# Pairs of expert tiles with the weights held in the array: a mixture-of-experts kernel on one Trainium2 core

## The chip, the core and the metric

The kernel runs on one core of a Trainium2 chip. The core has a matrix engine (TensorE, PE in the profile, whose weight loads are shown as PEld), a vector engine (VectorE, DVE), an activation engine (ScalarE, ACT), a general one (GpSimd, POOL) and SyncE (SP), which here only issues DMAs. The engines run side by side, each through its own queue in program order, and wait for each other by semaphores. Sixteen DMA engines move data between DRAM and SBUF, the on-chip memory of 128 partitions. TensorE writes to PSUM, which is used in banks of 128 x 512 fp32 values. The metric is the device time of one launch in microseconds, as the median of several runs.

## The reference

There are 4096 tokens of width 256, fp32 throughout. A layer norm feeds two branches, and x + both is the result.

```python
xn = _layernorm(x)
x = x + attention(xn, W_in, W_out) + moe(xn, ...)
# attention: Chebyshev features of q and k, running sums over the tokens
num = (Tq * kv_beta).sum(axis=3); den = (Tq.sum(axis=-1) * k_beta).sum(axis=3)
# moe
normed = layernorm(hidden, ln_w, ln_b); xf = normed.reshape(-1, 256)
logits = xf @ router_w                       # 8 experts
top_idx = argmax(logits); top_score = sigmoid(max(logits))
for e in experts:
    w = where(top_idx == e, top_score, 0.0)[:, None]
    xe = xf * w
    routed += (silu(xe @ g[e]) * (xe @ u[e])) @ d[e]      # 256 -> 512 -> 256
shared = (silu(xf @ sh_gate) * (xf @ sh_up)) @ sh_down
return hidden + routed + shared
```

Each token goes to one expert, and its score multiplies the rows before gate and up.

## The kernel before

The tokens form 8 chunks of 512, that is 32 tiles of 128 rows. The front (`front`) normalizes each chunk, writes the normalized rows to `z_dram`, and makes a transposed copy for the shared expert (`xfT`) and one for attention (`xnT`). `route` then finds each token's expert and a slot for it in a table: every expert's tokens fill whole tiles of 128 slots, and what is left over goes in quarters of 32 rows. With `NFULL = 26` whole tiles and `NPART = 31` quarters there are `NJ = 34` tiles, the last 8 of them quartered, and `NI = 57` sets of weights to load. The table holds, for each slot, the row to take from `z_dram` (`take_i`), the row of `y_dram` to write (`give_i`), and the score (`slot_s`).

`expert(n, j)` runs a tile. SyncE loads the gate, up and down weights of its expert, or of its four experts (L1173 to L1181, 512 KB each). GpSimd gathers the 128 rows by an indirect DMA (L1183). TensorE transposes them (L1191), ScalarE applies the layer norm's weight and bias on the way out of PSUM (L1194). Gate and up are matmuls in which the 128 rows lie in the array and 512 weight columns move (L1201), so they come out with the rows on the partitions. ScalarE's silu and VectorE's product (L1207, L1209) take the score as a factor per partition. The result is transposed in four blocks (L1214, L1216), so that the down product (L1222, 256 columns moving) can have it in the array. A copy (L1225 or L1226) and an indirect DMA (L1229) write the rows to `y_dram`. Quartered tiles keep four experts side by side in 32-column groups of the array.

`shared(c, gate)` is the shared expert on a chunk: L924 for gate and up with 512 columns moving, L933 for the product, L942 for down. It has the weights in the array and the tokens moving, so its intermediate result needs no transpose. `attend(c, gate)` is attention on a chunk: the qkv products (L987), a long chain of VectorE operations up to L1117, and the output product (L1125). At the end, SyncE loads `y_dram` back, chunk by chunk (L1251), VectorE adds it (L1260), and the result is stored (L1264). The loads of `y_dram` wait for all scatters.

The order on each engine is written out by a planner before the launch. Every operation is an `op` with an engine, a planned cost in us, what it reads and writes, buffers to allocate and a priority; `Plan.order` starts what is ready, by priority and by its planned clock, and emits it. A gather is planned with 1.28 us of GpSimd and a landing time, a scatter likewise; each scatter writes a key of its own:

```python
op("POOL", 1.28, f, r=[yt, "table"], w=[("y", j)], nbytes=128 * KiB, prio=SCAT)
```

The semaphores themselves are added afterwards by the framework, from the memory that the instructions touch. Buffers come from pools: `w_p` for weight sets (8 places, two more once the transposed copies of the front are free, and more once attention has ended), `zt_p` for gathered rows, `sl_p` and `hm_p` for the intermediate results, `bank_p` for six PSUM banks. `hold` ties the start of the last two shared chunks to the up products of given expert tiles.

Of the kernel before, what the change touches and what calls it, by code (L numbers as in the profile page):

```python
# [11 lines left out]
F32 = mybir.dt.float32  # L12
I32 = mybir.dt.int32
AF = mybir.ActivationFunctionType
ALU = mybir.AluOpType
AX = mybir.AxisListType
# [4 lines left out]
P = 128  # L21
NB, S, D = 2, 2048, 256
# [11 lines left out]

NFULL = NTT - 3 * NE // 4
NPART = 4 * NTT + NE - 1 - 4 * NFULL
NJ = NFULL + (NPART + 3) // 4
NI = NFULL + NPART  # L40
GP = 2
EPS = 1e-5
EPS_DEN = 1e-7
# [212 lines left out]
def kernel(  # L256
# [23 lines left out]

    z_dram = dram.tile([NTOK, D], F32, name="z_dram")
    y_dram = dram.tile([NTOK, D], F32, name="y_dram")
    ratio_dram = dram.tile([NTT, P], F32, name="ratio_dram")
    xn_dram = [dram.tile([P, KD, CH], F32, name=f"xn_dram_{c}") for c in range(NC)]
    xf_dram = [dram.tile([P, KD, CH], F32, name=f"xf_dram_{c}") for c in range(NC)]
# [52 lines left out]
    def cut(n):  # L338
        nonlocal at
        at += n  # L340
        return wide[:, at - n : at]
# [1 line left out]
    ratio_p = Pool([cut(CH) for _ in range(4)])  # L343
    route_at = at
    at = 0
    sl_p = Pool([cut(FF) for _ in range(3)])
    hm_p = Pool([cut(FF) for _ in range(2)])
    zt_p = Pool([cut(D) for _ in range(NZT)])
    xt_p = Pool([cut(D) for _ in range(2)])
    yt_p = Pool([cut(D) for _ in range(NYT)])  # L350
# [339 lines left out]
    def route():  # L690
# [3 lines left out]
        def t2(name, n=NTT, p=P):  # L694
            return cut(n)[:p]
# [4 lines left out]
        iota = t2("iota", P)  # L700
        top, idx, pos, tok1, score, hi = (t2(n) for n in ("top", "idx", "pos", "to", "sc", "hi"))
        quart = t2("quart", 4 * NTT)
        end = t2("en", NE)
        m, w = t3("m"), t3("w")
        iota_i = wide[:, at - NTT * NE : at - NTT * NE + P].bitcast(I32)
        tok = wide[:, at - NTT : at].bitcast(I32)
        tot, incl, gt = t3("tot", NTT, NE), t3("incl", NTT, NE), t3("gt", NTT, NE)
        le = t2("le", NI * NE, 1).rearrange("p (j e) -> p j e", e=NE)
        ej = t2("ej", NI, 1)
        full, odd, first, wh, lft, lend, base, jump = (t2(n, NE) for n in ("fu", "od", "fi", "wh", "lf", "le", "ba", "ju"))  # L710
        it_e = iota[:, :NE].unsqueeze(1).to_broadcast([P, NTT, NE])
        assert at <= wide.shape[-1]

# [61 lines left out]

        def f():
            V.tensor_reduce(odd, over, AX.X, ALU.add)
            V.tensor_reduce(full, over.rearrange("p e (t q) -> p e t q", q=4)[:, :, :, 3], AX.X, ALU.add)
        op("DVE", 1.6, f, r=["gt"], w=["full"], prio=R)

        def f():

            V.tensor_tensor_scan(end, ones[:, :NE], full, 0.0, ALU.mult, ALU.add)
            V.tensor_tensor(first, end, full, ALU.subtract)
            V.tensor_scalar(end, end, float(NFULL), None, ALU.min)
            V.tensor_scalar(first, first, float(NFULL), None, ALU.min)
            V.tensor_tensor(wh, end, first, ALU.subtract)
            V.scalar_tensor_tensor(lft, wh, -4.0, odd, ALU.mult, ALU.add)
            V.tensor_tensor_scan(lend, ones[:, :NE], lft, 0.0, ALU.mult, ALU.add)
        op("DVE", 1.4, f, r=["full", "gt"], w=["ends"], prio=R)  # L790

        def f():

            V.tensor_scalar(base, first, float(P), None, ALU.mult)
            V.tensor_tensor(lft, lend, lft, ALU.subtract)
            V.tensor_scalar(lft, lft, float(QD), float(NFULL * P), ALU.mult, ALU.add)
            V.tensor_scalar(wh, wh, float(P), None, ALU.mult)
            V.tensor_tensor(jump, lft, wh, ALU.subtract)
            V.tensor_tensor(jump, jump, base, ALU.subtract)
            V.tensor_tensor(incl, incl, tot, ALU.subtract)  # L800
        op("DVE", 1.4, f, r=["ends"], w=["start"], prio=R)

        def f():
            V.tensor_tensor(
                incl, rank.t[:, : NTT * NE].rearrange("p (t e) -> p e t", e=NE), incl, ALU.add,
            )
            V.tensor_tensor(gt, incl, wh.unsqueeze(2).to_broadcast([P, NE, NTT]), ALU.is_ge)
            V.tensor_tensor(gt, gt, jump.unsqueeze(2).to_broadcast([P, NE, NTT]), ALU.mult)
        op("DVE", 1.3, f, r=["start", rank], w=["slots0"], prio=R)

        def f():
            V.tensor_tensor(gt, gt, incl, ALU.add)
            V.tensor_tensor(
                w, gt.rearrange("p e t -> p t e"), base.unsqueeze(1).to_broadcast([P, NTT, NE]), ALU.add
            )
            V.tensor_tensor(w, w, m, ALU.mult)
        op("DVE", 1.2, f, r=["slots0", "m"], w=["slots"], prio=R)

        def f():
            V.tensor_reduce(pos, w, AX.X, ALU.add)  # L820
# [1 line left out]

        def f():

            for a, b, e in ((0, NFULL, end), (NFULL, NI, lend)):
                V.tensor_tensor(
                    le[:, a:b, :], e[0:1, :].unsqueeze(1).to_broadcast([1, b - a, NE]),
                    iota[0:1, : b - a].unsqueeze(2).to_broadcast([1, b - a, NE]), ALU.is_le,
                )
            V.tensor_reduce(ej, le, AX.X, ALU.add)  # L830
            V.tensor_scalar(ej, ej, float(NE - 1), None, ALU.min)
            V.tensor_copy(expert_i, ej)
# [59 lines left out]
        def f():  # L892
# [5 lines left out]
            V.scalar_tensor_tensor(u, table.t[:, :NJ], -0.75, u, ALU.add, ALU.add)  # L898
            V.tensor_copy(give_i, u)  # L899
        op("DVE", 1.1, f, r=[table, ("xn_dram", NC - 1)], w=["table"], prio=R)  # L900

    route()


# [238 lines left out]
    for i in range(2):  # L1143
        b = Buf(xfT_p, f"V_{i}")
        b.users = 1
        op("SP", 0.01, lambda: None, alloc=[b], prio=ROUTE, after=list(spilled),
           grow=lambda b=b: w_p.add([b.t]))
    for i, (q, n) in enumerate(((zt_p, D), (sl_p, FF), (hm_p, FF), (yt_p, D))):
        b = Buf(tv_p, f"U_{i}")
        b.users = 1  # L1150
        op("SP", 0.01, lambda: None, alloc=[b], prio=EXQ, after=lasts[-KD:],
           grow=lambda b=b, q=q, n=n: q.add([b.t[:, :n]]))
# [1 line left out]

    y_ins, downs, ups = [], [], []

    def expert(n, j):
        e = 0.1 * n

        parts = [(j, slice(0, P))]  # L1160
        if j >= NFULL:
            h = NFULL + 4 * (j - NFULL)
            m = min(4, NI - h)
            parts = [(h + i, slice(i * QD, (i + 1) * QD if i < m - 1 else P)) for i in range(m)]
        sets = [[Buf(w_p, f"{n}_{j}_{i}") for n in ("wg", "wu", "wd")] for i in range(len(parts))]
        wgs, wus, wds = ([s[i] for s in sets] for i in range(3))
        zt, xT, sl, hmT, yt = (Buf(q, f"{n}_{j}") for n, q in (
            ("zt", zt_p), ("xT", xt_p), ("sl", sl_p), ("hmT", hm_p), ("yt", yt_p)))
        pz, pg, pu, ph, py = (Buf(bank_p, f"{n}_{j}") for n in ("pz", "eg", "eu", "ph", "py"))
        ev = []  # L1170


        for n, src, cost in ((0, gate_w, 0.85), (1, up_w, 0.45), (2, down_w, 0.45)):  # L1173
            for i, (h, _) in enumerate(parts):
                def f(h=h, i=i, n=n, src=src, b=sets[i][n]):
                    if n == 0:
                        ev.append(nc.values_load(expert_i[0:1, h : h + 1], engines=[SP], min_val=0, max_val=NE - 1))
                    S_.dma_start(out=b.t.rearrange("p (k f) -> p k f", k=KF if n == 2 else KD),
                                 in_=src[ds(ev[i], 1)].rearrange("o (k p) f -> p (o k) f", p=P))
                downs.append(op("SP", cost, f, r=["experts"] + [("z_dram", n) for n in range(NC)], w=[sets[i][n]],  # L1180
                                alloc=[sets[i][n]], nbytes=512 * KiB, prio=EXQ + e, after=downs[-1:]))  # L1181

        op("POOL", 1.28, lambda: G.indirect_dma_start(  # L1183
            out=zt.t, out_offset=None, in_=z_dram,
            in_offset=bass.IndirectOffsetOnAxis(ap=take_i[:, j : j + 1], axis=0),
            bounds_check=NTOK - 1, oob_is_err=False,
        ), r=["table"] + [("z_dram", c) for c in range(NC)], w=[zt], alloc=[zt], nbytes=1024 * KiB, prio=EXQ + e - 0.05)

        def f():
            for k in range(KD):  # L1190
# [34 lines left out]
        op("ACT", 0.4, lambda: A.copy(yt.t, py.t[:, :D]), r=[py], w=[yt], alloc=[yt], prio=EXQ,  # L1225
           alt=[("DVE", 0.42, lambda: V.tensor_copy(yt.t, py.t[:, :D]))])  # L1226

        def f():
            y_ins.append(G.indirect_dma_start(  # L1229
                out=y_dram, out_offset=bass.IndirectOffsetOnAxis(ap=give_i[:, j : j + 1], axis=0),  # L1230
                in_=yt.t, in_offset=None, bounds_check=NTOK - 1, oob_is_err=False,
            ).ins)
        op("POOL", 1.28, f, r=[yt, "table"], w=[("y", j)], nbytes=128 * KiB, prio=SCAT)


    tiles = sorted(range(NJ), key=lambda j: j if j < NFULL else 3.2 * (j - NFULL) + 1.5)
    for n, j in enumerate(tiles):
        expert(n, j)

    gate, hold = [], {NC - 2: ups[-14], NC - 1: ups[-4]}
    for c in range(NC):
        gate = [shared(c, gate + ([hold[c]] if c in hold else spilled if c > 1 else []))]

# [1 line left out]
    for c in range(NC):  # L1247
        b = Buf(w_p, f"y_{c}")

        def f(c=c, b=b):  # L1250
            ins = S_.dma_start(  # L1251
                out=b.t.rearrange("p (t d) -> p t d", t=NT),
                in_=y_dram[c * CH : (c + 1) * CH].rearrange("(t p) d -> p t d", p=P),
            ).ins
            for s in y_ins:
                tc.add_manual_dep(ins, s.name, mybir.DependencyInfo(
                    mybir.DependencyClass.Sync, mybir.DependencyReason.DATA))
# [49 lines left out]
```

## Time and profile before

| quantity | value |
|---|---|
| median of 3 runs | 570.56 us (570.54 to 570.64) |
| the profiled execution | 570.69 us, of which the span 569.0 us |
| ScalarE | 238.0 us busy, 42% |
| VectorE | 486.2 us busy, 85%; 90 to 96% between 100 and 500 us |
| DMA | 132.67 MB, mean 233 GB/s |
| L1201, whole tiles from `big` (128*128, 512 moving) | 148 records, mean 595 ns |
| L1222, whole tiles from `big` (128*128, 256 moving) | 168 records, mean 387 ns |
| L1214, transposes of the intermediate result | 136 records with both forms, 276 ns |
| granted TensorE clock | 1.00 in the 28 stretches of 20 us up to 560 us, 0.95 after |

A mean of TensorE is the duration of one record, which includes the time through the array; neighbouring records overlap, so what one costs in a row of its kind is the distance from start to start, and the chain of work in order of time shows that. An fp32 matmul leaves two records. "Idle before, and its releaser" says how long an engine stood still ahead of an instruction, and which event ended that.

### The profile page before, as it was taken

What the parts mean: (1) busy time and instruction counts of PE and PEld (TensorE: products, weight loads), DVE (VectorE), ACT (ScalarE), POOL (GpSimd) and SP (SyncE); (2) the same over time, 40 slices, a digit from 0 to 9 for tenths busy, and PEclk for the clock granted to TensorE, in tenths of its full rate; (3) what the DMA queues carried; (4) which work ended last, traced back from release to release, by engine and by line L of the source; (5) the groups of instructions that cost most, each with busy time, mean ns of one, the idle gap of its engine ahead of it and who ended that gap; (6) DMA issues with size and microseconds to landing.
All of it is one profiled execution on the core that took longest, in us unless ns stands there. A gap on an engine that the chain in (4) does not pass through costs nothing.

```text
span 569.0 us, 8176 instructions
## 1 busy us (share of the span) xinstructions
PE 563.1 (99%) x2691; PEld 305.4 (54%) x2691; DVE 486.2 (85%) x799; ACT 238.0 (42%) x469; POOL 99.7 (18%) x113
## 2 busy tenths in 40 slices
PE   8999999999999999999999999999999999999997
PEld 7564555665535555464445455464555644553655
DVE  6899899999999999999899998999999999931254
ACT  4779662012553362354236435424733543311110
POOL 4211000005021102212120322215031321210100
PEclk9999999999999999999999999999999999999999
DMA  8857651336249918893884699299679938991089
GB/s 283 275 164 259 223 222 37 126 123 243 74 141 365 333 47 268 304 352 93 297 288 165 219 348 363 53 353 336 234 224 308 388 106 285 380 373 67 10 271 328
DMA packets 87689, 132.67 MB, mean 233 GB/s; under 512 B 5681, under 2 KB 52063, under 8 KB 87648
## 3 DMA queue, kind: packets, MB, share of 16 engines
q1 hardware_dynamic: 83152, 121.65, 62.7%
q0 software_dynamic: 3952, 10.51, 5.3%
q8 instruction: 21, 0.34, 0.3%
q14 instruction: 20, 0.16, 0.1%
q10 hardware_dynamic: 544, 0.00, 0.1%
HBM read 113.26 MB, written 19.15 MB: 233 GB/s over the span
## 4 chain that ended last, share of the span: by engine, by line
PE 98%; DVE 1%; DMA 0%; ACT 0%; issue 0%; DVEq 0%
PE bank L1201 22%; PE bank L924 20%; PE bank L987 15%; PE bank L1222 11%; PE bank L942 10%; PE bank L1125 5%; PE bank L1214 3%; PE psk L1017 3%; PE psq L1017 3%; PE bank L1191 1%; PE psk L1030 1%; PE bank L554 1%; PE psk L1111 1%; PE bank L874 1%; PE bank L587 1%; PE bank L1098 0%
## 5 line engine op out<-in xcount | busy, mean ns | idle before, releaser
L1201 PE MATMUL bank<-big,wide 128*32 128x512 f32 (+1 forms) x344 | 102.9, 596 | 0.0
L1229 POOL DMA_INDIRECT y_dram<-wide,give_i x32 | 41.4, 1293 | 304.1 <-ACT wide L1225 152.1
L987 PE MATMUL bank<-xnT,w_in 128*128 128x512 f32 x192 | 86.7, 594 | 0.0
L1054 DVE TENSOR_TENSOR_SCAN tv<-ones,carry,tv 128x512 f32<-128x512 f32 x60 | 76.6, 1277 | 1.2
L924 PE MATMUL bank<-xfT,sg 128*128 128x512 f32 (+1 forms) x136 | 61.1, 574 | 1.1 <-ACT xfT L532 1.1
L924 PE MATMUL bank<-xfT,su 128*128 128x512 f32 (+1 forms) x136 | 61.0, 573 | 0.0
L1201 PEld LDWEIGHTS bank<-big,wide 128*32 128x32 f32 (+1 forms) x344 | 34.6, 144 | 45.9 <-issue 42.1
L1183 POOL DMA_INDIRECT wide<-z_dram,take_i x34 | 42.9, 1262 | 85.5 <-DVE give_i L899 72.6
L942 PE MATMUL bank<-sd,hT 128*128 128x256 f32 x256 | 57.5, 379 | 0.0
L987 PEld LDWEIGHTS bank<-xnT,w_in 128*128 128x128 f32 x192 | 35.6, 190 | 39.0 <-issue 35.9
L1222 PE MATMUL bank<-big,wide 128*32 128x256 f32 (+1 forms) x352 | 54.2, 384 | 0.0
L942 PEld LDWEIGHTS bank<-sd,hT 128*128 128x128 f32 x256 | 48.0, 190 | 8.7 <-issue 2.5
L931 ACT ACTIVATE hT<-bank 128x512 f32<-128x512 f32 x32 | 19.0, 596 | 77.7 <-PE bank L924 73.5
L1222 PEld LDWEIGHTS bank<-big,wide 128*32 128x32 f32 (+1 forms) x352 | 37.0, 148 | 19.6 <-issue 7.5
L1207 ACT ACTIVATE wide<-bank,slot_s 128x512 f32<-128x512 f32 x33 | 22.6, 686 | 58.7 <-PE bank L1201 58.6
L1201 PE MATMUL bank<-xfT,wide 128*32 128x512 f32 (+1 forms) x100 | 45.6, 597 | 0.0
L1074 DVE TENSOR_TENSOR o<-o,tv 128x512 f32<-128x512 f32 x64 | 44.2, 690 | 1.7
L1209 DVE SCALAR_TENSOR_TENSOR wide<-bank,slot_s,wide 128x512 f32<-128x512 f32 x33 | 24.5, 743 | 17.9 <-PE bank L1201 17.5
L924 PEld LDWEIGHTS bank<-xfT,sg 128*128 128x128 f32 x136 | 24.6, 190 | 26.8 <-issue 24.1
L924 PEld LDWEIGHTS bank<-xfT,su 128*128 128x128 f32 x136 | 24.6, 190 | 25.3 <-issue 23.8
L1009 DVE SCALAR_TENSOR_TENSOR T<-T 128x1024 f32<-128x1024 f32 x32 | 38.1, 1220 | 0.0
L958 DVE TENSOR_TENSOR X<-X,bank 128x512 f32<-128x512 f32 x31 | 21.1, 679 | 15.6 <-PE bank L942 9.3
(224 smaller groups left out, 859.2 us busy)
## 6 DMA issues: line engine op xcount, KB each, us to landing
big<-in_gate_w SPq DMA_DIRECT2D x45, 512.0 KB
big<-in_down_w SPq DMA_DIRECT2D x44, 512.0 KB
big<-in_up_w SPq DMA_DIRECT2D x41, 512.0 KB
xfT<-in_up_w SPq DMA_DIRECT2D x14, 512.0 KB
xfT<-in_gate_w SPq DMA_DIRECT2D x11, 512.0 KB
xfT<-in_down_w SPq DMA_DIRECT2D x9, 512.0 KB
z_dram<-big SPq DMA_DIRECT2D x8, 512.0 KB
X<-in_x SPq DMA_DIRECT2D x7, 512.0 KB
```

The costliest lines, as they stand in the source:

```text
L924: T_.matmul(b.t[:, cols], wt[:, k, ts(f, P)], vx(k)[:, cols], start=(k == 0), stop=(k == KD - 1))
L942: T_.matmul(po.t[:, ts(i, D)], hT[f].t[:, ts(tp * 2 + i, P)], sd[:, f, :], start=(f == 0), stop=(f == KF - 1))
L987: T_.matmul(pm.t, w_in[:, k, ds(i * D + g * P, P)], xnT.t[:, ts(k, CH)], start=(k == 0), stop=(k == KD - 1))
L1009: op("DVE", 1.27, lambda i=i, j=j, q=part: V.scalar_tensor_tensor(q[i](), q[j](), off[i], q[1](), ALU.subtract, ALU.mult), r=[(T, j)] + X2 ...
L1017: T_.matmul(pt.t[ts(i - 1, QD), :], heads[:, 24 - g * HB : 24 - g * HB + QD], half[i](side), start=(g == 0), stop=(g == KD - 1 and (i > KD ...
L1054: o_ = op("DVE", 1.25, lambda b=b, i=i, g=g: V.tensor_tensor_scan(b.t, ones[:, 0:1].to_broadcast([P, CH]), b.t, 0.0 if opening else old[:, ...
L1074: op("DVE", 0.66, lambda o=o, b=b: V.tensor_tensor(o(), o(), b.t, ALU.add), r=[b, ok], w=[ok], prio=p)
L1125: T_.matmul(pa.t[:, ts(i, D)], o2.t[:, ds(g * CH + (tp * 2 + i) * P, P)], w_out[:, g, :], start=(g == 0), stop=(g == KD - 1))
L1183: op("POOL", 1.28, lambda: G.indirect_dma_start(out=zt.t, out_offset=None, in_=z_dram, in_offset=bass.IndirectOffsetOnAxis(ap=take_i[:, j ...
L1201: T_.matmul(b.t[n, :], xT.t[:, ds(k * P + n.start, n.stop - n.start)], wt.t[:, ts(k, FF)], start=(k == 0), stop=(k == KD - 1), skip_group_ ...
L1222: T_.matmul(py.t[n, :D], hmT.t[:, ds(i * P + n.start, n.stop - n.start)], wd.t[:, ts(i, D)], start=(i == 0), stop=(i == KF - 1), skip_grou ...
L1229: y_ins.append(G.indirect_dma_start(out=y_dram, out_offset=bass.IndirectOffsetOnAxis(ap=give_i[:, j : j + 1], axis=0), in_=yt.t, in_offset ...
```

## The change

Whole tiles are now of two kinds. `NPAIR = 9` pairs hold 256 rows of one expert, `NONE = 8` single tiles are left, the quarters stay 31: 9 + 8 + 31 = 48 weight sets. `pair(n, j)` gathers two tiles, transposes them into one bank, and has the weight blocks in the array with the 256 rows moving (L1256 of the changed file). Gate and up so come out transposed and go straight into the down product (L1269). As a row's score now lies along the free dimension, it can't be a factor per partition: the scores of the pairs are transposed once after routing (L926), stored to `score_dram` (L930), loaded for each pair spread over all partitions (L1230), and multiplied into the rows by VectorE before gate and up (L1246). A pair ends in one copy (L1272, L1273) and two scatters (L1211). Single and quartered tiles run through `expert` as before; gather, scatter and the weight loads have become functions. Routing has one more kind of slot to assign. `sl_p` and `hm_p` become one pool `h_p`; one of the two places that `w_p` got early goes to `h_p` and `zt_p` instead. The order of the units and the two `hold` points are new.

```diff
+NPAIR = (4 * NTT - 7 * NE) // 8
+NONE = NFULL - 2 * NPAIR
...
-NI = NFULL + NPART
+NI = NPAIR + NONE + NPART
...
-    sl_p = Pool([cut(FF) for _ in range(3)])
-    hm_p = Pool([cut(FF) for _ in range(2)])
+    h_p = Pool([cut(FF) for _ in range(5)])
...
+        rows = Buf(bank_p, "rows")
+        op("PE", MT, lambda: T_.transpose(rows.t[: 2 * NPAIR, :P], slot_s[:, : 2 * NPAIR], ident), r=["table"], w=[rows],
+           alloc=[rows], prio=R)
+        row = lambda: both.t[: 2 * NPAIR, 256 : 256 + P]
+        op("ACT", 0.25, lambda: A.copy(row(), rows.t[: 2 * NPAIR, :P]), r=[rows], w=[(both, "row")], prio=R)
+        op("POOL", 1.0, lambda: G.dma_start(out=score_dram, in_=row()), r=[(both, "row")], w=["score_dram"],
+           nbytes=8 * KiB, prio=R)
...
-           grow=lambda b=b: w_p.add([b.t]))
+           grow=lambda b=b, i=i: w_p.add([b.t]) if i else (
+               h_p.add([b.t[:, :FF]]), zt_p.add([b.t[:, ds(FF + n * D, D)] for n in range(2)])))
...
+    def scatter(j, yt, src):
+        def f():
+            y_ins.append(G.indirect_dma_start(
+                out=y_dram, out_offset=bass.IndirectOffsetOnAxis(ap=give_i[:, j : j + 1], axis=0),
+                in_=src(), in_offset=None, bounds_check=NTOK - 1, oob_is_err=False,
+            ).ins)
+        op("POOL", 1.28, f, r=[yt, "table"], w=[("y", j)], nbytes=128 * KiB, prio=SCAT)
+
+    def pair(n, j):
...
+        weights(e, [j // 2], [ws])
+        for i in range(2):
+            gather(e, j + i, zts[i])
+        op("POOL", 1.0, lambda: G.dma_start(
+            out=sc.t.rearrange("p (i q) -> p i q", i=2),
+            in_=score_dram[j : j + 2].unsqueeze(0).to_broadcast([P, 2, P])),
+           r=["score_dram"], w=[sc], alloc=[sc], nbytes=128 * KiB, prio=EXQ + e - 0.04)
...
+            V.tensor_tensor(v, v, sc.t.unsqueeze(1).to_broadcast([P, KD, 2 * P]), ALU.mult)
...
+            def mm(b, wt, h=h):
+                for f in range(2):
+                    for k in range(KD):
+                        T_.matmul(b.t[:, ts(f, 2 * P)], wt.t[:, ds(k * FF + (2 * h + f) * P, P)], xT.t[:, ts(k, 2 * P)],
+                                  start=(k == 0), stop=(k == KD - 1))
...
+            op("ACT", 0.62, lambda sl=sl, pg=pg: A.activation(sl.t, pg.t, AF.Silu), r=[pg], w=[sl], alloc=[sl],
+               prio=EXQ, table="silu")
+            op("DVE", 0.69, lambda sl=sl, pu=pu: V.tensor_tensor(sl.t, sl.t, pu.t, ALU.mult), r=[pu, sl], w=[sl],
+               prio=EXQ)
...
+            def f(i=i):
+                for f in range(KF):
+                    T_.matmul(py.t[:, ts(i, D)], sls[f // 2].t[:, ds(f % 2 * 2 * P + i * P, P)], wd.t[:, ts(f, D)],
+                              start=(f == 0), stop=(f == KF - 1))
...
+        op("ACT", 0.6, lambda: A.copy(yt.t, py.t), r=[(py, 0), (py, 1)], w=[yt], alloc=[yt], prio=EXQ,
+           alt=[("DVE", 0.69, lambda: V.tensor_copy(yt.t, py.t))])
+        for i in range(2):
+            scatter(j + i, yt, lambda i=i: yt.t[:, ts(i, D)])
...
-    tiles = sorted(range(NJ), key=lambda j: j if j < NFULL else 3.2 * (j - NFULL) + 1.5)
+    units = [(3 * i, expert, 2 * NPAIR + i) for i in range(NONE)]
+    units += [(3 * i + 1, pair, 2 * i) for i in range(NPAIR)]
+    units += [(3.1 * (j - NFULL) + 1.2, expert, j) for j in range(NFULL, NJ)]
...
-    gate, hold = [], {NC - 2: ups[-14], NC - 1: ups[-4]}
+    gate, hold = [], {NC - 2: ups[-10], NC - 1: ups[-3]}
```

## The prediction

> **What bounds the kernel now.** I read the page's busy shares first, then TensorE's waits, then the chain of work in order of time, and last the queue of GpSimd (POOL) and the end of the run, because the change moves work there.
>
> ```profile
> PE 563.1 (99%) x2691; PEld 305.4 (54%) x2691; DVE 486.2 (85%) x799; ACT 238.0 (42%) x469; POOL 99.7 (18%) x113
> PE 98%; DVE 1%; DMA 0%; ACT 0%; issue 0%; DVEq 0%
> ...
> PE bank L924 <- ACT xfT L532: 1.1, 1, 1.1
> PE bank L384 <- POOL ones L289: 1.1, 1, 1.1
> ```
>
> The two wait lines are all of TensorE's waits, and both lie in the first 9 us. After that TensorE never stands still until 565.3 us, so up to there the time is a sum of TensorE instructions. The chain in order of time prices them (start, us, what; an fp32 matmul leaves two records, a transpose one):
>
> ```profile
> 446.24 0.44 PE bank L1214 x4
> 446.68 0.22 PE bank L1191 x2
> 446.90 1.72 PE bank L1201 x4
> 448.62 0.44 PE bank L1214 x4
> 449.05 1.73 PE bank L1222 x8
> ```
>
> A matmul with 512 moving columns takes 1.72/2 = 0.86 us (longer runs: 0.858), one with 256 takes 1.73/4 = 0.4325, a transpose 0.109.
>
> The end is bound twice. The last expert matmul ends at 537.7; 6.9 us of L942 and 20.65 us of the last shared chunk (13.73 + 6.92) follow, to 565.3. Beside them runs this stream:
>
> ```profile
> 536.77 0.98 POOL L1229 DMA_INDIRECT y_dram<-wide,give_i  x1 [10.40 <-DVE wide L1226]
> 539.94 0.98 POOL L1229 DMA_INDIRECT y_dram<-tv,give_i  x1 [2.19 <-DMA y_dram<-wide,give_i]
> ...
> 542.57 1.47 SPq L1251 DMA_DIRECT2D T<-y_dram  x3
> ...
> 549.86 16.76 SPq L1264 DMA_DIRECT2D out<-X  x10
> ```
>
> All eight loads of y_dram wait for the last scatter; the 8.4 MB of loads and stores then fill the DMA engines (share 1.09 to 1.10, 348 to 387 GB/s) from 545 to 566.
>
> **The change, part by part.**
>
> TensorE, from the order in which both programs queue their instructions: gate and up lose 72 matmuls of 512 (72 x 0.858 = 61.8 us) and gain 144 of 256 (144 x 0.4325 = 62.3): +0.5. 72 transposes of L1214 go (-7.9), one comes for the scores (+0.1). A step from a 32-column tile to a full one costs about 0.19 more (L1222 x8 takes 1.93 there, not 1.73) and the step back 0.13; there are two fewer of each: -0.6. Sum **-7.9 us**, all on the path. [...]
>
> VectorE: routing gains 11 operations on 128x8 (0.17 each), one reduction (about 0.35) and 3 on 128x256 (0.42): +3.5. Up to its last attention product it also has 9 score products (0.66 each from start to start), 16 products of 0.61 for 16 of 0.66, three copies fewer, two shared products earlier: +5.3. That product ended at
>
> ```profile
> 500.80 0.75 DVE L1117 TENSOR_TENSOR o<-o,bank 128x256 f32<-128x256 f32 x2
> ```
>
> TensorE took it up 1.2 us later (502.7). With +8.8 it ends near 510, and TensorE, 7.9 us lighter but with 6.9 us of L942 and other work moved ahead of it, wants it near 508: 0 to 2.5 us of wait if nothing else delays TensorE. VectorE's own 22 us of waits between 20 and 502 can absorb it; I take 0, 2.5 goes into the range.
>
> ScalarE: fewer and wider activations, 42% busy, nothing. Weights: 27 loads of 512 KB fewer, but one weight place fewer too (9 before the late ones come, 10 before).
>
> GpSimd is where I expect the loss. Its queue runs in order. It gains nine score loads (0.55 us each by L499) and one score store, harmless by themselves. But a pair ends in **two scatters in a row**, and a scatter waits until the one before it has landed, as here:
>
> ```profile
> 376.46 1.84 POOL L1229 DMA_INDIRECT y_dram<-wide,give_i  x1 [6.69 <-ACT carry L1060]
> 384.21 1.00 POOL L1229 DMA_INDIRECT y_dram<-wide,give_i  x1 [5.90 <-DMA y_dram<-wide,give_i]
> ...
> DMA to landing us min/median/max: 2.1/6.1/7.4
> ...
> DMA to landing us min/median/max: 3.6/5.9/7.3
> ```
>
> The planner knows nothing of that wait: it charges 1.28 us for a scatter and gives each its own key. The two last lines are scatters and gathers. Where the DMA share after the issue is above 1.0, scatters land in 5.9 to 7.4 us, mostly 6.2; near 0.6 in 4.1 to 5.4; with idle DMA in 2.1 to 2.4. Gathers: 5.6 to 7.3, 4.2 to 5.2, 3.6.
>
> In the changed order the fifth to eighth pair's first gather stands right behind the second scatter of the pair before. From that pair's last matmul to the next pair's first transposes TensorE has only: a quartered tile's up 1.85, spreading 0.3, transposes 0.22, one shared gate 1.72, transposes 0.44, three qkv products 5.15, the quartered tile's down 1.9 = 11.6 us (11.5 to 11.8 at the four places). The chain needs: wake-up and copy 0.85, scatter 1.27, its landing 6.2, scatter 1.27, gap 0.3, gather 1.05, its landing 4.8 = 15.7. So TensorE stands still 4.1 us, four times: **+16.4**. I take 6.2 for the scatter since the quartered tile's four down weights (2 MB) and the next units' sets are being loaded just then, and 4.8 for the gather since that load is running out. All contended (6.2, 6.0): 16.9, or +21. Half (4.5, 4.5): +8. Idle (2.2, 3.6, short issues): 10, nothing. Behind the waiting scatter also stand other scatters and score loads; none is needed sooner than the gather.
>
> [...]
>
> The end: the last unit is now a pair, and 6.9 us of L942 have moved ahead of its last matmul, T0. T0 to the last TensorE instruction is 20.65. The copy (0.69) and wake-up take 0.95, the first scatter and its landing 0.98 + 2.19, the second 0.98, its landing 1.65 as before: first y load at T0 + 6.8 (before: + 4.8). From first y load to the span's end took 569.0 - 542.57 = 26.4; about 0.5 of it was the last two stores waiting for L949, which now come in time: 25.9. So the span ends at T0 + 32.7; TensorE's own path would be T0 + 24.4.
>
> Sum: TensorE ends at 565.3 - 7.9 + 16.4 = 573.8, T0 = 553.2, span 585.9. The profiled execution took 570.69 against a span of 569.0, so 1.7 lies around it: **587.6 us**; that execution is 0.1 above the median of 570.56. I say 587.
>
> **The rivals.**
>
> 1. Only the end counts: the gathers arrive in time (idle DMA, or the 10% less traffic). T0 = 565.3 - 7.9 - 20.65 = 536.8, span 569.5, time 571.2; with VectorE's 2.5 us 573.7. For: POOL is 18% busy and no gather was late before. Against: the DMA share at such moments.
> 2. On the faster side: the two scatters of a pair do not wait for each other. They come from one tile, a form no row shows. Then neither stall exists and the end is 3.2 us shorter: 536.8 + 29.5 + 1.7 = 568.0. It decides when the end after T0 is under 30.9. Against: every scatter that followed another closely in the trace waited.
> 3. Weight places run short: a quartered tile wants eight at once for gate and up, and one of nine still holds the pair's down. One 512 KB load late (1.5 us at 348 GB/s) in each of eight rounds is +12 on top: about 599.
>
> That the change does not do what it says is excluded by the instruction counts.
>
> **How the numbers follow.** Forecast 0.62, with 4 x 2 to 4 x 5.3 us of stalls: 579 to 593. Rival one 0.18, rival two 0.10, rival three 0.10. The range must take in rival one and the forecast's contended end: 570.5 to 596. Within 0.2% (569.4 to 571.7), about what a measurement here can tell from no change, lies a part of rival one: 0.06. Faster is rival two and a little: 0.11. Slower 0.83.
>
> **What would show it.** Right: TensorE idle before the transposes of four pairs, some 4 us each, released by the gather; GpSimd waiting some 6 us before each second scatter; about 12 us between the last matmul and the end, before 3.7; matmuls of 256 at 0.43. Wrong: second scatters without a wait, TensorE without idle time, or idle time released by weight loads or VectorE.

## The result and the profile after

The changed kernel takes **579.41 us** (median of five runs, 579.15 to 582.9) against 570.64 us for the kernel before beside it (570.54 to 571.5): a ratio of **1.0168**, 95% interval 1.0138 to 1.0197. The forecast was 587. The profiled execution is the slowest of the five, 582.9 us with a span of 581.1, and so 3.5 us longer than the median. Sums below are made against its own span.

The busy shares of the changed kernel, and all of TensorE's waits after the first 9 us (line waited at, releaser: us in total, times, longest):

```profile
PE 556.4 (96%) x2764; PEld 325.2 (56%) x2764; DVE 491.7 (85%) x820; ACT 223.2 (38%) x429; POOL 103.4 (18%) x123
...
PE bank L1237 <- DMA xfT<-z_dram,take_i: 6.8, 3, 4.0
PE bank L1237 <- DMA wide<-z_dram,take_i: 1.6, 1, 1.6
```

TensorE is busy for 6.7 us less than before, and yet it ends later: it now waits four times, 8.4 us in all, each time at a pair's first transposes (L1237), each time for a gather. What GpSimd did ahead of the longest of these waits stands in its queue in order of time (start, us, what, idle time before and its releaser):

```profile
386.76 1.10 POOL L1211 DMA_INDIRECT y_dram<-xfT,give_i  x1 [14.30 <-ACT xfT L1272]
394.15 1.35 POOL L1211 DMA_INDIRECT y_dram<-xfT,give_i  x1 [6.29 <-DMA y_dram<-xfT,give_i]
395.80 1.61 POOL L1203 DMA_INDIRECT xfT<-z_dram,take_i  x1 [0.30 <-issue]
```

The second scatter of a pair waits 6.29 us for the landing of the first. The gather behind it had nothing to wait for itself (0.30 us, "issue") and simply left late. On TensorE the same stretch reads:

```profile
402.18 0.41 PE L1237 MATMUL bank<-ident,xfT 128*128 128x128 f32 x2 [4.03 <-DMA xfT<-z_dram,take_i]
402.42 2.62 PE L1305 MATMUL bank<-big,wide 128*128 128x512 f32 x4
404.83 0.63 PE L1295 MATMUL bank<-ident,wide 128*128 128x128 f32 x2
405.25 2.69 PE L1256 MATMUL bank<-wide,xfT 128*128 128x256 f32 x8
407.78 0.60 PE L1318 MATMUL bank<-ident,wide 128*128 128x128 f32 x4
408.21 1.89 PE L1256 MATMUL bank<-wide,big 128*128 128x256 f32 x8
```

The wait is 4.03 us, and then the work is slower: two groups (L1305 x4, L1256 x8) that take 1.88 and 1.89 us elsewhere take 2.62 and 2.69. More on that in the last section.

The end, first TensorE's chain, then the loads and stores on SP's queue:

```profile
543.53 3.45 PE bank L1269 x16
546.98 8.60 PE bank L955 x20
```

```profile
553.14 0.37 SPq L1352 DMA_DIRECT2D T<-y_dram  x1
553.62 2.33 SPq L1352 DMA_DIRECT2D big<-y_dram  x3
556.05 5.75 SPq L1352 DMA_DIRECT2D T<-y_dram  x4
561.89 13.39 SPq L1365 DMA_DIRECT2D out<-X  x10
```

The last expert matmul (L1269) ends at 547.0, the first load of y is issued 6.2 us later, and the span ends 28.0 us after that. TensorE's last matmul ended at 567.7, so 13.4 us follow in which VectorE ends its additions (until 570.9) and the stores go out; before, 3.7 us followed.

### The profile page after: what moved, and what is told of

Read it like the earlier page. It is cut to its first block, busy times and chain, and to the rows that moved or that the text cites. A ratio compares the mean times of both kernels' runs of the same rounds, so it can differ in the third digit from the quotient of the medians.

```text
span 581.1 us, 8153 instructions
## 1 busy us (share of the span) xinstructions
PE 556.4 (96%) x2764; PEld 325.2 (56%) x2764; DVE 491.7 (85%) x820; ACT 223.2 (38%) x429; POOL 103.4 (18%) x123
## 4 chain that ended last, share of the span: by engine, by line
PE 43%; issue 9%; DMA 6%; POOL 1%; ACT 1%; DVE 1%; POOLq 0%
PE bank L1256 7%; PE bank L1305 7%; PE bank L1018 6%; PE bank L955 5%; PE bank L1269 4%; PE bank L1326 4%; PE bank L1156 4%; DMA xfT<-z_dram,take_i 3%; PE bank L973 2%; DMA T<-y_dram 2%; PE psk L1048 1%; PE psq L1048 1%; POOL y_dram L1211 1%; DMA wide<-z_dram,take_i 1%; DMA y_dram<-wide,give_i 1%
## 5 line engine op out<-in xcount | busy, mean ns | idle before, releaser
L1018 PE MATMUL bank<-xnT,w_in 128*128 128x512 f32 x192 | 87.1, 594 | 0.0
L1211 POOL DMA_INDIRECT y_dram<-wide,give_i x32 | 38.3, 1198 | 205.8 <-ACT wide L1329 49.6
L1305 PE MATMUL bank<-big,wide 128*32 128x512 f32 (+2 forms) x280 | 63.3, 602 | 0.0
L973 PE MATMUL bank<-sd,hT 128*128 128x256 f32 x256 | 58.0, 381 | 0.0
L1018 PEld LDWEIGHTS bank<-xnT,w_in 128*128 128x128 f32 x192 | 35.4, 190 | 36.7 <-issue 34.5
L973 PEld LDWEIGHTS bank<-sd,hT 128*128 128x128 f32 x256 | 47.8, 190 | 9.5 <-issue 3.2
L1203 POOL DMA_INDIRECT wide<-z_dram,take_i x20 | 26.3, 1317 | 110.7 <-DVE wide L921 78.7
L1305 PEld LDWEIGHTS bank<-big,wide 128*32 128x32 f32 (+2 forms) x280 | 18.4, 128 | 30.3 <-issue 29.5
L964 DVE TENSOR_TENSOR hT<-hT,bank 128x512 f32<-128x512 f32 x32 | 21.8, 683 | 16.1 <-PE bank L955 15.1
L1091 ACT COPY carry<-tv 128x1 f32<-128x1 f32 x80 | 15.1, 189 | 49.7 <-DVE tv L1085 49.2
L1082 DVE TENSOR_TENSOR tv<-T 128x512 f32<-128x512 f32 x48 | 32.4, 674 | 0.1
L1026 ACT ACTIVATE T<-bank 128x512 f32<-128x512 f32 x32 | 19.0, 596 | 30.8 <-PE bank L1018 30.6
L1256 PE MATMUL bank<-wide,big 128*128 128x256 f32 x128 | 30.4, 382 | 0.0
```

Of the source, the lines that this page charges most:

```text
L973: T_.matmul(po.t[:, ts(i, D)], hT[f].t[:, ts(tp * 2 + i, P)], sd[:, f, :], start=(f == 0), stop=(f == KF - 1))
L1018: T_.matmul(pm.t, w_in[:, k, ds(i * D + g * P, P)], xnT.t[:, ts(k, CH)], start=(k == 0), stop=(k == KD - 1))
L1082: V.tensor_tensor(b.t, q[i](1), v(), ALU.mult)
L1203: op("POOL", 1.28, lambda: G.indirect_dma_start(out=zt.t, out_offset=None, in_=z_dram, in_offset=bass.IndirectOffsetOnAxis(ap=take_i[:, j ...
L1211: y_ins.append(G.indirect_dma_start(out=y_dram, out_offset=bass.IndirectOffsetOnAxis(ap=give_i[:, j : j + 1], axis=0), in_=src(), in_offse ...
L1256: T_.matmul(b.t[:, ts(f, 2 * P)], wt.t[:, ds(k * FF + (2 * h + f) * P, P)], xT.t[:, ts(k, 2 * P)], start=(k == 0), stop=(k == KD - 1))
```

## Experiments

Ten runs, each against the kernel before on the same chip (570.72 to 570.74 us).

| run | what differs from the changed kernel | median us | range |
|---|---|---|---|
| changed kernel | | 579.41 | 579.15 to 582.9 |
| e1_told | planner knows that a scatter waits for the last one | 575.90 | 574.82 to 577.27 |
| e2_side | a pair's second scatter goes to another tensor | 571.42 | 570.88 to 571.6 |
| e3_hold | shared chunk later | 575.40 | 573.85 to 575.72 |
| e4_both | e1_told and e3_hold | 570.27 | 569.15 to 572.41 |
| e5_told6 | e4_both, scatters planned to land in 6 us | 570.66 | 570.3 to 571.6 |
| e6_side_hold | e2_side and e3_hold | 567.86 | 567.06 to 568.48 |
| e7_no_scores | score loads and products left out | 581.08 | 580.04 to 581.95 |
| e8_told6_no_scores | the same on e5_told6 | 569.61 | 569.56 to 569.91 |
| e9_told6_end | e5_told6, last ten scatters as before | **565.88** | 565.58 to 566.17 |
| e10_told5_end | e9_told6_end with 5 us | 567.71 | 567.38 to 568.51 |

**The wait between a pair's scatters, taken away.** A second DRAM tensor removes what makes the second scatter wait; every instruction and the queue's order stay. The final loads read `z_dram`, so the experts' sum is left out of the result (the diff is shortened to its changed lines).

```diff
-                out=y_dram, out_offset=bass.IndirectOffsetOnAxis(ap=give_i[:, j : j + 1], axis=0),
+                out=y_dram if dst is None else dst, out_offset=bass.IndirectOffsetOnAxis(ap=give_i[:, j : j + 1], axis=0),
...
-            scatter(j + i, yt, lambda i=i: yt.t[:, ts(i, D)])
+            scatter(j + i, yt, lambda i=i: yt.t[:, ts(i, D)], y2_dram if i else None)
...
-                in_=y_dram[c * CH : (c + 1) * CH].rearrange("(t p) d -> p t d", p=P),
+                in_=z_dram[c * CH : (c + 1) * CH].rearrange("(t p) d -> p t d", p=P),
```

> The second scatter of each pair writes to a second DRAM tensor that nobody reads, and the final loads read z_dram in place of y_dram (the sum of the experts' rows is left out); instructions, sizes and queue order stay. Only the wait of a pair's second scatter for its first is gone. Theory: the gathers behind leave about 5 us sooner, TensorE's 8.4 us of waits fall under 1.5, and at the end the first load starts 1.7 us sooner after the last expert matmul: 568 to 573 us. Rival A (the wait is not what makes the gather late): 577 to 580 us, of which only the 1.7 us at the end is gained.

571.42 us, in the expected range. The stretch of GpSimd's queue that held the longest stall now reads (the view names both tensors y_dram):

```profile
382.45 1.10 POOL L1212 DMA_INDIRECT y_dram<-xfT,give_i  x1 [14.30 <-ACT xfT L1273]
383.85 0.98 POOL L1212 DMA_INDIRECT y_dram<-xfT,give_i  x1 [0.30 <-issue]
385.14 1.04 POOL L1204 DMA_INDIRECT xfT<-z_dram,take_i  x1 [0.30 <-issue]
```

After its first 9 us TensorE has one wait left in this run's trace:

```profile
PE bank L1019 <- DVE X L990: 0.3, 1, 0.3
```

All four waits for gathers are gone with the wait of the pairs' second scatters. TensorE's last group (L974, 7.07 us) starts at 550.34, so it ends at 557.4. That is the kernel before's 565.3 less 7.9, the sum that the prediction made from matmul prices.

**The same by order.** One key tells the planner of the dependence that the framework adds; it then puts the next pair's first gather between the two scatters.

```diff
-        op("POOL", 1.28, f, r=[yt, "table"], w=[("y", j)], nbytes=128 * KiB, prio=SCAT)
+        op("POOL", 1.28, f, r=[yt, "table"], w=[("y", j), "landed"], nbytes=128 * KiB, prio=SCAT)
```

> The order of GpSimd alone is changed: the planner is told that a scatter starts only when the one before it has landed, so that at the four places with a stall the next pair's first gather stands between the two scatters of the pair. Theory (the gather is late because it stands behind a scatter that waits): the gathers leave some 5 us sooner, TensorE's waits before the transposes fall from 8.4 us to under 1, the clock stays at 1.00 around 400 us, TensorE ends near 558 and the time is 569.5 to 574 us. Rival A (a gather is late of itself, by its landing or by its place coming free): the waits stay, 578 to 581 us. Rival B (VectorE is next late): a wait of 1 to 3 us before the last output product, released by VectorE, 573 to 576 us.

575.90 us, above the range: half a repair. GpSimd's queue in this run:

```profile
382.47 1.25 POOL L1211 DMA_INDIRECT y_dram<-xfT,give_i  x1 [11.70 <-ACT xfT L1272]
384.03 1.04 POOL L1203 DMA_INDIRECT xfT<-z_dram,take_i  x1 [0.30 <-issue]
389.18 1.00 POOL L1211 DMA_INDIRECT y_dram<-xfT,give_i  x1 [4.11 <-DMA y_dram<-xfT,give_i]
395.72 1.86 POOL L1211 DMA_INDIRECT y_dram<-wide,give_i  x1 [5.54 <-ACT wide L1311]
397.89 1.06 POOL L1203 DMA_INDIRECT xfT<-z_dram,take_i  x1 [0.31 <-issue]
```

The first gather now goes at 384.03, in the shadow of the first scatter. But the planner believes a scatter to land in 2.7 us, and a third scatter, of another tile, came to stand ahead of the next gather (397.89). The view puts its wait down to an ACT operation that ended at 395.1; the landing of the second scatter, 5.8 us after its start, came within 0.2 us of that. TensorE waits 2.2 us for the gather:

```profile
PE bank L1237 <- DMA xfT<-z_dram,take_i: 2.2, 1, 2.2
...
PE bank L1318 <- DVE wide L1313: 1.0, 1, 1.0
```

With 1.7 us of slow matmuls behind it that makes 4.9 us; the last expert matmul comes 4.6 us later than in e2_side.

**The end.** In the changed kernel 6.9 us of L973 had moved ahead of the last expert matmul. The point that holds the last but one shared chunk is moved:

```diff
-    gate, hold = [], {NC - 2: ups[-10], NC - 1: ups[-3]}
+    gate, hold = [], {NC - 2: ups[-8], NC - 1: ups[-3]}
```

> Only the point at which the last but one shared chunk may start is moved, from the tenth last up to the eighth last: by the order of TensorE's queue 29.3 us of its work then follow the last expert matmul, in place of 20.7, and the last output product of attention is wanted 5 us earlier. The stalls stay. Theory (the end is set by the loads and stores of y that start at the last expert matmul): this matmul comes 8.6 us sooner, the span ends some 34 us after it, now about 4 us after TensorE's own end: 571 to 574 us. Rival A (the end follows TensorE, so that the length of work behind the last expert matmul is immaterial): 579 us. Rival B (VectorE then holds TensorE back at the last output product, by up to 5 us): 575 to 578 us.

575.40 us: the theory's direction, but short of its range and inside that of rival B. The last expert matmul ends at 540.1 and the span 4.4 us after TensorE, so the tail is repaired; part is given back in attention, where TensorE now waits 1.1 us for VectorE at L1142 and 0.5 at L1318 (rival B's mechanism, but 1.6 us instead of up to 5, and not at the output product) and runs slowly for 3.4 us afterwards.

**Both.** 

> Both edits, the order of the scatters and the later shared chunk. If both theories hold, TensorE ends near 557.5, the last expert matmul near 528.5, and the time is 562 to 565 us, below the kernel before by the 7.9 us of the transposes less about 1. If VectorE is then late at the last output product (it ended at 514.5 in the changed kernel and would end near 508 without stalls, wanted near 505), TensorE waits 3 to 5 us there and the time is 566 to 569 us. If neither edit reaches the path: 579 us.

570.27 us: a gain of 9.1, somewhat more than the two single gains together (3.5 and 4.0), and no better than the kernel before. It lies outside all ranges given; the second branch, 566 to 569, is the nearest. TensorE's waits: 2.1 us for the gather behind the third scatter again, and 2.9 for VectorE at four places, of which only 0.6 at the output product (L1156) that the branch had named.

**Scatters planned as they land.** Charging 1024 KiB for a scatter (as the planner does for a gather) makes it expect 5.9 us.

> The later shared chunk, and the planner told of the scatters as of the gathers: a scatter starts when the one before has landed, and that takes some 6 us. By the resulting order no gather that is wanted soon stands behind a waiting scatter, and 31.0 us of TensorE's work follow the last expert matmul. If the chain of scatters is the whole cause of the stalls, TensorE waits under 1 us for gathers, ends near 558 to 560 and the run takes 564 to 566.5 us, faster than the kernel before by about 0.9%. If VectorE is next (it held TensorE for 2.9 us in all in the run with both edits), 567 to 569 us. If the gathers are late for another reason too, the wait of 2.1 us before the eighth pair stays and the time is 569 to 571 us.

570.66 us, the number of the third branch but not its reason: the trace shows a success spoiled at the end. No gather is waited for, TensorE ends at 559.7, but the span at 568.5. VectorE's queue:

```profile
549.46 0.69 DVE L964 TENSOR_TENSOR hT<-hT,bank 128x512 f32<-128x512 f32 x1 [2.74 <-PE bank L955]
550.07 1.22 DVE L1361 TENSOR_TENSOR X<-X,big 128x1024 f32<-128x1024 f32 x1
```

The loads of y were issued from 534.88 on; the first addition (L1361) stood behind a shared product that had to wait for TensorE. The planner had believed the last scatters late and had placed the addition accordingly; the stores began at 551.3.

**The same with the last ten scatters charged as before**, and a second order with 768 KiB as a control (5.0 us by the planner's own formula; the expectation says 4.9). Both have the later shared chunk:

```diff
-        op("POOL", 1.28, f, r=[yt, "table"], w=[("y", j)], nbytes=128 * KiB, prio=SCAT)
+        op("POOL", 1.28, f, r=[yt, "table"], w=[("y", j), "landed"], nbytes=(1024 if len(puts) < 24 else 128) * KiB, prio=SCAT)
+        puts.append(j)
```

> As the run with 6 us told to the planner for each scatter, but only for the first 24 of the 34; the last ten are charged as before. In that run TensorE ended at 559.7, yet the span 8.8 us later: the planner, believing the last scatters late, had put the first addition of y behind three other operations of VectorE, so that the stores began at 551.3. Here that addition comes after one of them. If that was all, the stores begin near 544, the span ends 4.2 to 4.5 us after TensorE (558.5 to 560), and the time is 564.5 to 566.5 us, faster than the kernel before by 0.7 to 1.1%. If the end is bound by something else: 569 to 571 us.

> The same with the scatters charged at 4.9 us in place of 5.9: another order of GpSimd's queue with the same intent, to tell whether the gain hangs on one lucky order. If the gathers' place behind waiting scatters is the cause, this order too has at most one wait for a gather of some 2 us: 564.5 to 568.5 us. If the other order was luck: 570 to 575 us.

565.88 us, ratio 0.9910 (0.9896 to 0.9924), and 567.71 us, 0.9948 (0.9935 to 0.9962): both faster than the kernel before, with two different orders, neither with a wait for a gather. Of the 1.5 us between their profiled executions, 1.0 lies in TensorE's end (560.0 and 561.0), where the second waits 2.3 us for VectorE at L1319 and the first 0.3, in part offset by other waits; the rest lies behind TensorE. In e9_told6_end TensorE ends at 560.0 and the span at 563.9; its largest wait after the start is

```profile
PE psk L1142 <- DVE rec L1134: 0.9, 1, 0.9
```

and the stores begin right behind the loads:

```profile
542.98 18.34 SPq L1366 DMA_DIRECT2D out<-X  x10
```

**No scatter wait, and the later chunk**, as a bound.

> No wait between a pair's scatters (second one to a tensor that nobody reads, the final loads read z_dram in place of y_dram, so that the experts' sum is left out) and the later shared chunk. It bounds what the two repairs can give together. Theory: no wait for gathers, TensorE ends near 557.5 plus what VectorE holds it up in attention (1 to 3 us), 4.4 us to the end of the span, 1.7 around it: 564 to 567 us. If VectorE held TensorE back by as much as it is late by its own count (5 us): 568 to 569.

567.86 us, between the two ranges: no gather is late. In the profiled execution (567.06 us) TensorE ends at 561.5, held up 1.9 us in all by VectorE and by 1.7 us of slow matmuls. e9_told6_end goes below this supposed bound, with TensorE's end 1.5 us sooner. The slow matmuls do not explain that: the other four executions of this run have a mean granted clock of 1.000, where the profiled one has 0.997, and they took longer, 567.85 to 568.48 us. So this run bounds its own order of work only, and what e9's order does better stays open.

**VectorE and the score loads.**

> The changed kernel without the loads of the scores and their product on VectorE (the pairs' rows go unscaled); the planned order stays. Theory (VectorE and these loads lie beside the path; the scatters' wait and the end set the time): 578 to 580.5 us, the four waits before the transposes as before. Rival (the nine products and loads cost what VectorE and GpSimd spend on them, 6 us and 5 us): 573 to 576 us.

> As the run with 6 us told to the planner, again without the score loads and products (the pairs' rows go unscaled). If VectorE is the next bound once the stalls are gone, this run is 1 to 3 us faster than that one; if TensorE's own work and the end are, the two agree within 0.6 us.

581.08 us, a little above the expected range and no faster than the changed kernel: all four waits before the transposes remain (1.05, 2.00, 1.19 and 1.81 us; two put down to the gather, two to a copy on ScalarE). Nine products and nine loads are beside the path there. With the stalls gone (e8_told6_no_scores: 569.61 against 570.66 us) they are worth 1.05 us. In the traces TensorE ends 0.7 us sooner and its wait of 0.6 us for VectorE at L1142 is gone. So VectorE is next by this wait, though not by the 6 us that the products take on it; the run takes loads and products out together and does not part them further.

## Why the prediction was right, and where its sizes were off

- **TensorE's sum, -7.9 us**: right. e2_side, without stalls, ends at 557.4, 7.9 earlier. The trace prices the new form as the row of L1222 did, half a matmul of 512 columns: 1.73/4 = 0.43 us against 1.72/2 = 0.86. L1222 and L942 of the kernel before have this shape too, 256 columns moving, with a weight load of 190 ns for each record, and take the same 0.43. Chain of the changed kernel:

```profile
244.95 1.72 PE bank L955 x4
...
250.32 1.73 PE bank L1256 x8
```

- **VectorE at 0**: right in effect, wrong in size. No wait for it is in the trace of the changed kernel. Its last attention product was to end near 510; in e2_side, where nothing else delays it, it ends at 504.3.
- **GpSimd's queue, four stalls, +16.4 us**: mechanism, places and releaser are as forecast, and removing the scatter's wait (e2_side) or passing it (e9_told6_end) removes the stalls. The size was off: 8.4 us. The step that failed is the sum of the chain, 15.7 us at each place: it adds issue and landing, 1.27 + 6.2 for the first scatter and 1.05 + 4.8 for the gather, but the profile counts a landing from the start of the issuing instruction, so the issue is in it already. The eighth pair shows that. Its first scatter starts at 386.76, issues for 1.10 and lands after 7.1 us by the profile's view of that instruction. From the start that is 393.9, just before the second scatter goes at 394.15; from the end of the issue it would be 395.0, too late for it. With each issue counted once, the chain is 13.4 us and the stall 1.8, four times: +7.3, and the forecast about 578. Start to start, read from GpSimd's and TensorE's timelines, with the landings by the same view:

| us | predicted | 5th pair | 6th | 7th | 8th |
|---|---|---|---|---|---|
| first to second scatter | 7.47 | 5.86 | 5.13 | 6.24 | 7.39 |
| of it the landing, from the start | 6.2, and the issue again | 5.6 | 4.9 | 6.0 | 7.1 |
| second scatter to gather | 1.57 | 1.72 | 1.70 | 1.28 | 1.65 |
| gather to transposes | 5.85 | 4.37 | 5.74 | 5.48 | 6.38 |
| of it the landing, from the start | 4.8, and the issue again | 4.2 | 5.6 | 5.3 | 6.2 |
| sum | 14.89 | 11.95 | 12.57 | 13.00 | 15.42 |
| TensorE waits | 4.1 | 0.80 | 1.58 | 1.99 | 4.03 |

  Sum less wait, the work that TensorE had in hand, is 11.0 to 11.4 at all four places against 10.75 forecast. The landings themselves were well chosen on average (5.9 for 6.2, 5.3 for 4.8). Only the eighth pair waited as long as worked out, and that is luck: its landings were 0.9 and 1.4 us longer than assumed and made up for the issues counted twice. The DMA share between the scatters was 0.76 at the first place and 1.02 to 1.07 at the other three, where the landings took 4.9 to 7.1 us; the share does not order them. Available time and chain lie so close together that such a spread makes a stall of 0.8 us or of 4.0.
- **Not foreseen**: 1.7 us lost at half clock after the longest stall (granted 0.50 from 404 to 406).
- **The end**: T0 to the span's end was put at 32.7 and is 34.1. The first load came 0.6 sooner than forecast; from it to the end went 28.0, not 25.9. SP's queue waited 2.3 us for places between the loads, and the DMA share is 0.88 between 555 and 560, where the kernel before has 1.10 between 545 and 550. That this is the whole cause is not shown: e2_side waits only 0.9 us for places and takes 28.2, with a DMA share of only 0.06 to 0.11 from 566 to 568.
- **Rivals**: weight places short: no wait for weights is in the trace. Scatters that don't wait: excluded by GpSimd's timeline, where the four second scatters waited 4.1 to 6.3 us. Only the end counts (571.2): excluded by the four waits for gathers. e2_side comes to that number, but by luck. In it the scatters of a pair do not wait, so it is the case of rival two, 568.0. Its last expert matmul ends at 536.8 as that rival has it; its end took 32.9 us from there, not 29.5.

Against the span: 569.0 - 7.9 + 8.4 + 1.7 + 9.7 (13.4 in place of 3.7 behind TensorE) = 580.9; measured 581.1. Against the forecast for that execution (587.6) the errors partly cancel: the stalls were put 8.0 too high, the end 1.4 too low, and the slow clock was left out (1.7). The range, 570.5 to 596, was wide enough to take in rival one as well.

## What to carry to other kernels

The two scatters of a pair write disjoint rows of one DRAM tensor, and still the second waited for the first: 4.1 to 6.3 us at the four places with a stall, 0.3 us at the eighth pair when it went to another tensor (e2_side). What stood behind it paid for that landing, with 8.4 us of TensorE's time in all. A planner that does not know this dependence puts the wrong thing there. Tell it the dependence with a landing time taken from the trace, and look where its late estimates then move other queues: here the first repair gained 3.5 us and the last, with the later chunk, 13.5. Before a landing time goes into a sum, find out from which event the profile counts it. And when the last unit of work grows, move filler work behind it: the end cost 9.7 us of the span, more than the stalls' 8.4.

## What the runs showed of the hardware

In the changed kernel a stall of TensorE cost more than its own length: 4.03 us of wait, and 1.7 us of slow work behind it. The windows around that wait (stretch, sum, busy time of PE, PEld, DVE, ACT and POOL, then granted clock, DMA share, GB/s):

```profile
398.00:400.00 2.00, 0.15 (x1) 0.00 (x0) 1.67 (x2) 0.88 (x2) 0.00 (x0) 1.00 1.02 391
400.00:402.00 2.00, 0.00 (x0) 0.00 (x0) 0.00 (x0) 0.00 (x0) 0.96 (x1) 1.00 1.07 363
402.00:404.00 2.00, 1.82 (x6) 0.87 (x7) 0.00 (x0) 0.00 (x0) 1.18 (x3) 0.86 1.05 387
404.00:406.00 2.00, 2.00 (x6) 1.29 (x5) 0.85 (x2) 0.50 (x2) 0.51 (x1) 0.50 1.04 390
406.00:408.00 2.00, 2.00 (x10) 1.63 (x10) 1.93 (x4) 0.31 (x1) 0.00 (x0) 0.79 1.06 385
408.00:410.00 2.00, 2.00 (x13) 1.79 (x12) 2.00 (x3) 1.44 (x4) 0.00 (x0) 1.00 1.07 388
```

The granted clock falls to 0.50 about 1.3 us after work has resumed, and is back at 1.00 some 3.4 us later; the work takes 1.7 us more (from the start of L1305 to the start of L1318 5.36 us here, 3.66 in e3_hold). Shorter waits came before the same drop: in e6_side_hold the clock fell after two waits of 0.51 and 1.13 us, 1.6 us in all (of PE's busy time, granted clock, DMA share, GB/s):

```profile
427.50:430.50 3.00, 1.41 (x21) 0.97 1.01 332
430.50:433.50 3.00, 3.00 (x5) 0.50 1.08 380
433.50:436.50 3.00, 3.00 (x8) 0.96 1.07 370
```

In e3_hold the same two waits (0.50 and 1.13 us) were followed by half clock too, 0.50 from 438.5 to 441.5. In e4_both the same two were followed by no slow work: the nine records of L1018 right behind them took 4.13 us, where ten took 6.22 in e3_hold. Nor did a wait of 2.96 us in e3_hold change the clock (1.00 from 400 to 410). So the length of a wait alone does not order these cases. No run here moved a wait on purpose, and what decides stays open. A drop may be a part of the changed kernel's spread of 3.7 us, where e9_told6_end, without a drop in its profile, spreads over 0.6; that is not shown, and in e6_side_hold the execution with the drop is the fastest.
